# Three graph layers on one core: root products, late node blocks, lots and the last run are placed anew

## The chip, the cores and the metric

The kernel runs on one core of one Trainium2 chip. The metric is the device time of one execution in microseconds (us); the figure before is the median of three runs.

## The reference

A graph with 6250 nodes of 256 features and 100000 edges, sorted by destination. Destinations are crowded at low node numbers (`dst = 6250 * u**2`). Each edge has 32 attributes and one of three types. Three layers are computed, and a layer norm of the input plus the result stands at the end:

```python
ew = edge_attr @ edge_w + edge_b                      # 100000 x 256, the same for all layers
for l in range(3):
    msg = relu(x[src] * ew)
    out = 0
    for i in range(3):                                # mean over the edges of each type
        h = segment_sum(msg * (edge_type == i), dst) / max(count_i, 1)
        out = out + h @ weights[l, i]
    x = x + relu(out + x @ roots[l] + biases[l])
result = layernorm(x_in + x)
```

## The kernel before, in words

**Edges.** 256 edges make a pair (two tiles of 128), two pairs a quad; there are 391 pairs, numbered in the order of destinations. For each tile POOL issues one indirect gather, which fetches the 128 source rows into `xs` (L1378). A quad of rows has one of eight buffers (`ROWS = 8`). DVE multiplies a quad by the edge weights (`weigh`, L838), ACT applies relu (L839), DVE makes one-hot tiles of the destinations (`one_hot`, L852), and PE sums the rows into PSUM with them (`reduce`, L870 and L878). Consecutive pairs whose destinations fit into a window of 40 nodes form a run. A long run is first summed in the other orientation and turned (`take`, `turn`: the "turned" runs), and DVE adds each run to the accumulator `acc` (`add`, L918).

**Layer by layer.** Layer one also computes the edge weights on PE (`make_ew`, L815). It stores them for the later layers (`keep_ew`, L765 and L771), and it sorts the rows of the first 52 pairs by source block: each such tile is scattered by an indirect DMA from POOL to a table in memory (`scatter`, one after each later gather, L733). Layers two and three don't gather these 52 pairs. They read the table back in 39 "lots" (three types by 13 groups of four node blocks), whose source rows PE picks out of `x_all` in SBUF (`choose`, `expand`, L794, L801). A lot takes a quad's two steps and no gather.

**Nodes.** The nodes form 49 blocks of 128. When all of a block's edges are in `acc`, three products with the relation weights follow (`node_mul`, L947, in two parts), DVE scales and adds them (`node_end`, L978, L981) and SP writes the block to `x_mid` (L984). ACT clears its place in `acc`. The product with the root matrix comes earlier: `root_turn`, `root_turned`, `root_mul`, `root_keep` at steps s, s+2, s+3 and s+6 (L923, L927, L931, L934), into one of 22 slots (`ROOTS`). In the last layer a block is also normalised and stored (`deviate`, `norm`).

**Order.** `layer` is one loop over steps `it`. Each step emits work of many stages: the gather of pair `it + 9`, the product of pair `it + 3`, the reduction of pair `it`, and node work by table. Each engine executes its instructions in the order of emission and waits on semaphores, so POOL can run ahead of the other engines as far as buffers and scatters let it. `order_of` puts the pairs in order: 76 to 390 (with the sorted quads, or the lots, mixed in by `places_of`), then 75 down to 58, which belong to node block 1. `stages` says at which step each run is taken, turned and added; `schedule` gives `starts[c]`, the step in which block c's node products begin. Block 1 begins last, after the last run.

**Between layers.** The next layer gathers from `x_mid`. Its first six pairs (12 gathers, `gather_early`) are ordered so that they need all blocks but block 1, whose rows `complete` adds by a matmul. They are emitted after the last gather of a layer. From the seventh pair on, gathers read all of `x_mid`, block 1 included.

Of the kernel before, what the change touches and what calls it, by code (L numbers as in the profile page):

```python
# [442 lines left out]
def ordered_path(ctx, tc, x, attr_laid, A, weights, roots, biases, edge_w, edge_b, out, src, src_i, seg, place_i, consts, x_root,  # L443
# [8 lines left out]
    N, D = x.shape  # L452
    E = src.shape[0]
    L, R = weights.shape[:2]
# [230 lines left out]
    def layer(l, r_sb, b_sb, ats, early, pools):  # L685
# [5 lines left out]
        steps = len(order)  # L691
        soon = min(SOON, steps - max(starts[:1] + starts[2:]) - 5)
        taken, turns, added, banks = stages(N, E, share, l)
# [315 lines left out]

        node_at = {s: c for c, s in enumerate(starts)}  # L1010
        turns_of = [node_at[s] for s in sorted(node_at)]
        at_root = {c: (j + 2 * FIRST) % ROOTS for j, c in enumerate(turns_of)}
        root_at = {}

        for j, c in enumerate(turns_of):
            step = max(3 + int((steps - 110) * (1 - (1 - j / NT) ** 0.5)), max(root_at, default=-1) + 6)
            if j >= ROOTS:
                step = max(step, starts[turns_of[j - ROOTS]] + 5)
            assert step + 8 <= starts[c]
            root_at[step] = c  # L1020
# [6 lines left out]
        if l == L - 1:  # L1027
# [6 lines left out]
            for c in turns_of:  # L1034
                step = max(used[c], max(given_at, default=0) + 2)
                assert step <= starts[c] + 2, (c, step, starts[c])
                given_at[step] = c
        for it in range(-11, max(starts) + 8):
# [69 lines left out]
            if it - 2 == moved:  # L1108
                clear(P)
            if it - 2 in node_at:  # L1110
                node_end(node_at[it - 2], 0)
            if it - 4 in node_at:
                node_end(node_at[it - 4], 1)
                if node_at[it - 4] == 1:
                    node_end(1, 2)
                clear(slot_of(node_at[it - 4]))
            if it + 1 in node_at and slot_of(node_at[it + 1]) == 0:
                wrap()
            if it in node_at:
                node_mul(node_at[it], 0)  # L1120
            if it - 2 in node_at:
                node_mul(node_at[it - 2], 1)
                if node_at[it - 2] == 1:
                    node_mul(1, 2)
            if it - 5 in node_at and l == L - 1:
                deviate(node_at[it - 5])
            if it - 6 in node_at and l == L - 1:
                norm(node_at[it - 6])
            if pair(2) is not None and first_of(it + 2, 2) and pair(2) // 2 != order[-1] // 2:
# [44 lines left out]
LOT_AT = 6  # L1174
LOT_SPACE = 4.5
LOT_MORE = 0.04
LOT = 4
# [46 lines left out]
def places_of(N, E):  # L1224

    K = first_pairs(N, E)
    quads = [K + ZONE_AT + int(ZONE_SPACE * j) for j in range(zone_of(N, E) // 2)]
    lots = [K + LOT_AT + int(LOT_SPACE * j + LOT_MORE * j * j) for j in range(len(lots_of(N)))]
    return [w + w % 2 for w in quads], [w + w % 2 for w in lots], K + MIDDLE_AT


def spans_of(N, E):
# [6 lines left out]
    quads, lots, middle = places_of(N, E)  # L1239
    stops = {K, last, middle, *quads, *lots}  # L1240
    node = lambda e: N * min(1.0, e / E) ** 2
# [47 lines left out]
def stages(N, E, share, l):  # L1289
# [15 lines left out]
    for k, group in enumerate(groups):  # L1305
        done = closes[group[-1]]
        late = k + 2 < len(groups)
        some = any(turned(spans[n], last) for n in group)
        by = min(opens[groups[k + 2][0]] - 1, done + (4 if some else 3)) if late else 0
        by = max(by, done + 1 + some)  # L1310
        for j, n in enumerate(group):
# [6 lines left out]
            elif late and j < len(group) - 1:  # L1318
                added[s] = max(done + 1, by - 1)
    return taken, turns, added, banks  # L1320


def schedule(N, E, share, l):
# [23 lines left out]
    for c in range(2, NT):  # L1347
        if starts[0] is None and ready <= max(done[c] + 2, step + 4):
            step = starts[0] = max(ready, step + 4)
        step = starts[c] = max(done[c] + 2, step + 4)  # L1350
    if starts[0] is None:
# [214 lines left out]
```

## Time and profile before

| | us |
|---|---|
| median of three runs (2900.62 to 2906.98) | 2903.43 |
| profiled execution | 2903.96 |
| its span, first to last instruction | 2902.2 |
| gathers and scatters on POOL, number | 2242 |
| POOL busy | 2138.6 |
| PE busy | 2409.1 |
| DVE busy | 2207.5 |
| ACT busy | 1708.1 |
| mean granted TensorE clock | 0.948 of full speed |

In the rows that follow, a row of the timeline gives the start of an instruction in us from the start of the span, its duration, engine, line, operation, destination and source, and in brackets how long the engine had been idle before it and what released it. A row of the windows gives a stretch, its length, and for each engine the busy time with the number of instructions, then the granted clock. A row of the waits gives the total, the count and the longest.

### The profile page before, as it was taken

The page shows a single profiled execution, that of the slowest core. Times are in us where ns is not written, and L with a number is a line of the kernel's source. Part 1 is how long each engine was busy: PE and PEld are TensorE (multiplying, and loading weights), DVE is VectorE, ACT ScalarE, POOL GpSimd, SP SyncE. Part 2 cuts the span into 40 slices and gives each one's busy share as a digit, 9 for nine tenths or more (in the row PEclk, how much of TensorE's full clock was granted, in tenths as well). Part 3 has the DMA queues.
Part 4 walks back from the last instruction along what each step waited for, and adds up shares of the span by engine and source line. Part 5 has one row for each costly group of instructions (what it writes and reads, how often), then busy time and mean ns, then how long its engine had stood idle before and what let it go on. Part 6 is the DMA issues. An engine that isn't in the chain of part 4 may idle for free. (4 is left out here: it accounts for less than half of the span.)

```text
span 2902.2 us, 44132 instructions
## 1 busy us (share of the span) xinstructions
PE 2409.1 (83%) x13302; PEld 1880.6 (65%) x13302; DVE 2207.5 (76%) x5612; ACT 1708.1 (59%) x2220; POOL 2138.6 (74%) x2253
## 2 busy tenths in 40 slices
PE   5799988888988789788898888777888888878776
PEld 2466656555666566577777777665666767767665
DVE  7777766766656576677878888776788888888986
ACT  5677766666666667455655555444555555555654
POOL 7676777777777775777777777776777777767775
PEclk9899998999889999999999999898999999999998
DMA  7898665556555666887777777676777777777765
GB/s 237 280 328 272 207 198 190 189 185 196 185 192 187 196 211 202 267 262 240 256 242 243 246 237 257 215 223 195 269 255 262 255 256 240 244 227 233 249 227 156
DMA packets 285411, 668.25 MB, mean 230 GB/s; under 512 B 50555, under 2 KB 142509, under 8 KB 285165
## 3 DMA queue, kind: packets, MB, share of 16 engines
q1 hardware_dynamic: 170112, 362.98, 35.9%
q0 software_dynamic: 107616, 294.11, 33.9%
q10 hardware_dynamic: 7436, 8.24, 0.9%
q8 instruction: 110, 1.80, 0.3%
q14 instruction: 137, 1.11, 0.1%
HBM read 528.50 MB, written 136.63 MB: 229 GB/s over the span
## 5 line engine op out<-in xcount | busy, mean ns | idle before, releaser
L1378 POOL DMA_INDIRECT xs<-x_mid,src_r x1332 | 1265.3, 950 | 420.1 <-issue 343.1
L1378 POOL DMA_INDIRECT xs<-in_x_dram,src_io x770 | 734.9, 954 | 243.1 <-issue 211.8
L839 ACT ACTIVATE xs<-xs 128x1024 f32<-128x1024 f32 x533 | 559.5, 1050 | 582.8 <-DVE xs L838 561.0
L838 DVE TENSOR_TENSOR xs<-ew_p,xs 128x1024 f32<-128x1024 f32 x533 | 646.5, 1213 | 314.3 <-ACT keep L771 176.3
L878 PE MATMUL h_p<-oh,xs 128*128 128x120 f32 x4768 | 692.5, 293 | 202.7 <-DVE acc L918 105.4
L878 PEld LDWEIGHTS h_p<-oh,xs 128*128 128x128 f32 x4768 | 641.3, 203 | 304.9 <-DVE acc L918 112.4
L852 DVE TENSOR_SCALAR oh<-iota_w,seg_o 128x120 f32<-128x120 f32 x2138 | 568.2, 328 | 0.0
L870 PE MATMUL h_p<-xs,oh 128*120 128x256 f32 x1868 | 517.7, 405 | 41.5 <-issue 14.7
L947 PE MATMUL o_p<-w_sb,acc 128*128 128x256 f32 (+1 forms) x1752 | 456.1, 397 | 64.8 <-DVE x_root L978 56.6
L918 DVE TENSOR_TENSOR acc<-h_p,acc 128x240 f32 (+1 forms) x764 | 338.9, 445 | 113.5 <-PE o_p L947 45.7
L947 PEld LDWEIGHTS o_p<-w_sb,acc 128*128 128x128 f32 (+1 forms) x1752 | 323.6, 195 | 141.5 <-DVE x_root L978 73.9
L870 PEld LDWEIGHTS h_p<-xs,oh 128*120 128x120 f32 x1868 | 319.5, 189 | 146.6 <-issue 30.0
L786 ACT ACTIVATE ew_p<-ew_s 128x1024 f32<-128x1024 f32 (+1 forms) x340 | 343.3, 1010 | 12.7 <-DMA ew_s<-ew_all 12.7
L771 ACT ACTIVATE keep<-ew_p 128x1024 f32<-128x1024 f32 x170 | 173.2, 1019 | 226.1 <-issue 115.5
L978 DVE SCALAR_TENSOR_TENSOR x_root<-o_p,inv,x_root 128x256 f32<-128x256 f32 (+1 forms) x438 | 210.5, 480 | 43.0 <-PE o_p L947 36.1
L839 ACT ACTIVATE zone<-zone 128x1024 f32<-128x1024 f32 (+1 forms) x78 | 78.8, 1010 | 223.9 <-DVE zone L838 223.9
L815 PE MATMUL ew_p<-ew_sb,at 64*128 64x512 f32 x630 | 199.0, 710 | 11.8 <-ACT ew_p L789 11.7
L789 ACT ACTIVATE ew_p<-seed 128x1024 f32<-128x1024 f32 (+1 forms) x194 | 198.5, 1023 | 0.0
L931 PE MATMUL r_p<-r_sb,t_s 128*128 128x256 f32 x588 | 158.7, 392 | 21.7 <-ACT t_s L927 21.4
L838 DVE TENSOR_TENSOR zone<-ew_p,zone 128x1024 f32<-128x1024 f32 (+1 forms) x78 | 90.6, 1162 | 107.5 <-PE ew_p L801 107.3
L870 PE MATMUL h_p<-zone,oh 128*120 128x256 f32 x576 | 148.0, 387 | 11.6 <-DVE acc L918 7.0
L801 PE MATMUL ew_p<-x_all,hot 128*128 128x256 f32 x588 | 150.6, 401 | 7.6 <-DVE hot L794 7.4
(178 smaller groups left out, 2340.8 us busy)
## 6 DMA issues: line engine op xcount, KB each, us to landing
ew_s<-ew_all SPq DMA_DIRECT2D x338, 512.0 KB
ew_all<-keep SPq DMA_DIRECT2D x169, 512.0 KB
zone<-zone_table SPq DMA_DIRECT2D x72, 516.0 KB
xs<-x_mid,src_r POOLq DMA_INDIRECT x1332
zone_table<-blank SPq DMA_DIRECT2D x21, 677.2 KB
xs<-in_x_dram,src_io POOLq DMA_INDIRECT x770
x_mid<-x_all SPq DMA_DIRECT2D x96, 128.0 KB
at<-in_attr_laid_dram SPq DMA_DIRECT2D x40, 256.0 KB
```

Source lines behind the costliest of these rows:

```text
L786: nc.scalar.activation(ew_ps[q][:, :n], ew_ss[q][:, :n], AF.Copy)
L789: nc.scalar.activation(ew_ps[q][:, :n], seed[:, None, None, :].to_broadcast([P, n, 2, D]), AF.Copy)
L815: nc.tensor.matmul(ew_ps[q][:, k].rearrange("p i d -> p (i d)"), at[half, :], ew_sb[half].rearrange("p i d -> p (i d)"), start=False, stop ...
L838: nc.vector.tensor_mul(there, ew_ps[q][:, pairs.start:pairs.stop, :n], there)
L839: nc.scalar.activation(there, there, AF.Relu)
L852: nc.vector.tensor_scalar(ohs[q][:, i, :], iota_w[:, :, :WIN], at, None, op0=ALU.is_equal)
L870: nc.tensor.matmul(h_p[:WK, :D], ohs[u // 2][:, t, :], rows_of(u, i), start=(i == 0 and first), stop=(i == n - 1 and closes(u)), skip_grou ...
L878: nc.tensor.matmul(h_p[:, d * WK:(d + 1) * WK], rows_of(u, i)[:, d * P:(d + 1) * P] if d < DC else full_ones, (ohs if d < DC else oh_bs)[u ...
L918: nc.vector.tensor_tensor(there, h_ps[span][:, :CH * WK].rearrange("p (c r w) -> p c r w", c=CH, r=R), there, op=ALU.add)
L947: nc.tensor.matmul(o_p[:n, j, :], acc[:, d, r, slot:slot + n], w_sb[:, r * DC + d, :], start=(d == 0), stop=(d == DC - 1))
L978: nc.vector.scalar_tensor_tensor(root, o_p[:n, j, :], inv[:n, c, r:r + 1], root, op0=ALU.mult, op1=ALU.add)
L1378: nc.gpsimd.indirect_dma_start(out=xs[:, u % 2, i, :], out_offset=None, in_=x_rows[:, :], in_offset=bass.IndirectOffsetOnAxis(ap=src_i[:, ...
```

## The change

1. In layer one the root products are no longer placed at steps 5, 11, 17, ... 293 (every six), but at 20, 27, 34, ... 356 (every seven). The other two layers keep their rule.
2. The last five blocks (`QUICK = 5`, blocks 44 to 48) take one step instead of two between the parts of their node work (`paces`): part 0 at s, part 1 and the first end at s+1, the second end, the clearing and the write at s+2. Their starts may stand three steps apart instead of four (366, 369, 372, 375, 378 in layer one, where they stood at 366, 370, 374, 378, 382; 388, 392, 396, 399, 402 in the other two, before 388, 393, 397, 401, 405). Block 48 starts at step 378 instead of 382 in layer one and ends at 380 instead of 386; in layers two and three it starts at 402 instead of 405 and ends at 404 instead of 409.
3. The lots, up to the 26th at the same places within a few pairs, thin out after that: the last 13 stood at places 226 to 310 (226, 232, 240, 246, 254, 260, 266, 274, 282, 288, 296, 304, 310) and come to 230 to 342 (230, 238, 244, 252, 260, 270, 278, 288, 296, 306, 318, 330, 342). Block 0, which needs all lots, starts at step 352 instead of 319 in layers two and three.
4. The last run, 7 pairs (58 to 64), is cut into one of two pairs (58, 59) and one of six (60 to 65), which is turned. In layers two and three both are added at step 415 (before: 414), and block 1 starts at 416 instead of 415. The run of pair 390 is added as soon as it is complete.

```diff
@@ ordered_path, layer
-        soon = min(SOON, steps - max(starts[:1] + starts[2:]) - 5)
+        soon = min(SOON, steps - starts[0] - 5, *(steps - starts[c] - 2 * paces(c, NT) - 1 for c in range(2, NT)))
...
         node_at = {s: c for c, s in enumerate(starts)}
+        next_at = {s + paces(c, NT): c for s, c in node_at.items()}
+        over_at = {s + 2 * paces(c, NT): c for s, c in node_at.items()}
...
         for j, c in enumerate(turns_of):
-            step = max(3 + int((steps - 110) * (1 - (1 - j / NT) ** 0.5)), max(root_at, default=-1) + 6)
+            step = ROOT_AT + ROOT_EVERY * j if l == 0 else 3 + int((steps - 110) * (1 - (1 - j / NT) ** 0.5))
+            step = max(step, max(root_at, default=-1) + 6)
...
-            if it - 2 in node_at:
-                node_end(node_at[it - 2], 0)
-            if it - 4 in node_at:
-                node_end(node_at[it - 4], 1)
-                if node_at[it - 4] == 1:
+            if it in next_at:
+                node_end(next_at[it], 0)
+            if it in over_at:
+                node_end(over_at[it], 1)
+                if over_at[it] == 1:
                     node_end(1, 2)
-                clear(slot_of(node_at[it - 4]))
+                clear(slot_of(over_at[it]))
...
-            if it - 2 in node_at:
-                node_mul(node_at[it - 2], 1)
-                if node_at[it - 2] == 1:
+            if it in next_at:
+                node_mul(next_at[it], 1)
+                if next_at[it] == 1:
                     node_mul(1, 2)
-            if it - 5 in node_at and l == L - 1:
-                deviate(node_at[it - 5])
-            if it - 6 in node_at and l == L - 1:
-                norm(node_at[it - 6])
+            if it - 1 in over_at and l == L - 1:
+                deviate(over_at[it - 1])
+            if it - 2 in over_at and l == L - 1:
+                norm(over_at[it - 2])
...
-LOT_SPACE = 4.5
-LOT_MORE = 0.04
+LOT_RATE = 0.215
+LOT_SLOWER = 0.000264
+ROOT_AT = 20
+ROOT_EVERY = 7
+QUICK = 5
@@ places_of
-    lots = [K + LOT_AT + int(LOT_SPACE * j + LOT_MORE * j * j) for j in range(len(lots_of(N)))]
+    lots = [K + LOT_AT + int((LOT_RATE - (LOT_RATE ** 2 - 4 * LOT_SLOWER * j) ** 0.5) / (2 * LOT_SLOWER))
+            for j in range(len(lots_of(N)))]
@@ spans_of
-    stops = {K, last, middle, *quads, *lots}
+    stops = {K, last, last + 2, middle, *quads, *lots}
@@ stages
+        if spans[group[-1]][1] == -(-E // 256):
+            by = 0
         by = max(by, done + 1 + some)
+def paces(c, NT):
+
+    return 1 if c >= NT - QUICK else 2
@@ schedule
-        step = starts[c] = max(done[c] + 2, step + 4)
+        step = starts[c] = max(done[c] + paces(c, NT), step + 2 + paces(max(c - 1, 2), NT))
```

More of the change, by code (lines that the diff above doesn't have):

```diff
@@ L1035, in layer @@
                 step = max(used[c], max(given_at, default=0) + 2)
-                assert step <= starts[c] + 2, (c, step, starts[c])
+                assert step <= starts[c], (c, step, starts[c])
                 given_at[step] = c
```

## The prediction

> **What bounds the kernel now.** I read the page first, then POOL's waits, then its timeline where it stands still, and last the windows of the other engines there.
>
> ```profile
> span 2902.2 us, 44132 instructions
> POOL 7676777777777775777777777776777777767775
> L1378 POOL DMA_INDIRECT xs<-x_mid,src_r x1332 | 1265.3, 950 | 420.1 <-issue 343.1
> L1378 POOL DMA_INDIRECT xs<-in_x_dram,src_io x770 | 734.9, 954 | 243.1 <-issue 211.8
> ...
> 2880.84 0.95 POOL L1378 DMA_INDIRECT xs<-x_mid,src_r  x1 [0.30 <-issue]
> 2882.09 0.95 POOL L1378 DMA_INDIRECT xs<-x_mid,src_r  x1 [0.30 <-issue]
> ```
>
> PE has the most busy time, but POOL sets the pace: a gather lasts 0.95 us, the next follows 0.30 us later whatever the rest does, so one starts every 1.25 us, and a pair costs POOL 2.50 us. The sevens in POOL's slices are this pace (0.95/1.25 = 0.76). The 2242 gathers and scatters would fill 2242 x 1.25 = 2803 us. The first 4 us and the 20 us from the last gather's start (2882.09) to the end make 2827; the other 75 us of the span are gaps beyond 0.30 and a few longer gathers. The change removes no gather, so only the gaps and the end can give anything.
>
> ```profile
> 96.67 0.95 POOL L1378 DMA_INDIRECT xs<-in_x_dram,src_io  x1 [0.30 <-issue]
> 105.04 0.94 POOL L1378 DMA_INDIRECT xs<-in_x_dram,src_io  x1 [7.43 <-issue]
> ...
> 293.82 1.00 POOL L733 DMA_INDIRECT zone_table<-keep,slot_i  x1 [11.48 <-ACT keep L765]
> ...
> 1141.30 0.95 POOL L1378 DMA_INDIRECT xs<-in_x_dram,src_io  x1 [0.30 <-issue]
> 1159.06 0.94 POOL L1378 DMA_INDIRECT xs<-x_mid,src_e  x1 [16.81 <-DMA x_mid<-x_all]
> ...
> 1174.06 0.94 POOL L1378 DMA_INDIRECT xs<-x_mid,src_r  x1 [0.30 <-issue]
> ...
> 2007.43 0.95 POOL L1378 DMA_INDIRECT xs<-x_mid,src_r  x1 [0.30 <-issue]
> 2017.61 0.95 POOL L1378 DMA_INDIRECT xs<-x_mid,src_e  x1 [9.23 <-issue]
> ...
> 2032.60 0.95 POOL L1378 DMA_INDIRECT xs<-x_mid,src_r  x1 [0.30 <-ACT ew_p L786]
> ```
>
> Four gaps make 45 us: two in layer one's first tenth (a full set of row buffers, then the first scatter, which needs the edge weights of the first sorted quad) and one at each change of layer, where the early gathers wait for block 48 in memory. The rest, about 14 us, lies in layer three:
>
> ```profile
> 2300.00:2440.00 140.00, 119.62 (x667) 99.99 (x667) 118.18 (x299) 80.79 (x119) 105.87 (x113) 1.00 0.77 250
> 2440.00:2620.00 180.00, 145.37 (x923) 128.09 (x923) 156.16 (x403) 97.13 (x129) 125.56 (x133) 0.98 0.73 240
> ```
>
> 133 gathers in 180 us are 1.35 us each, against 140/113 = 1.24 just before: 180 - 133 x 1.25 = 14 us stood still.
>
> **Root products of layer one: 5 us.** The first scatter hangs on ACT's `keep_ew` for the quad at step 100, emitted at step 96. Up to there 16 root products were emitted (steps 5 to 95); now there are 11 (20 to 90). The stretch is close to PE's limit:
>
> ```profile
> 90.00:106.00 16.00, 5.48 (x17) 2.73 (x15) 8.07 (x30) 3.47 (x4) 6.73 (x8) 0.61 0.59 199
> 106.00:282.00 176.00, 161.78 (x845) 107.21 (x843) 137.77 (x365) 133.99 (x182) 132.30 (x140) 0.99 0.92 302
> ...
> L931 PE MATMUL r_p<-r_sb,t_s 128*128 128x256 f32 x588 | 158.7, 392 | 21.7 <-ACT t_s L927 21.4
> L923 PE MATMUL r_p<-ident_o,x_all x294: 270/273/475, 54.1 to 2676.9; 128*128 128x128 f32 x147
> ```
>
> A block takes 158.7/147 = 1.08 us of products and two overlapping transposes, at most 0.4 more by their 0.27 each. Five fewer save up to 5 x 1.4 = 7 us of PE before the scatter. PE is busy 162 of 176 us, and three of the five stand ahead of the stall at 90 to 106, so I take 5, with 0 and 7 as ends. The gap before the scatter shrinks from 11.5 to about 6 us. The nine products that now come at steps 300 to 356 (9 x 1.4 = 13 us of PE) lie beside scatters, where a pair costs POOL more; only the last two meet a full PE (below).
>
> **Late blocks and the first change of layer: 5 us, not 17.** What does the gap of 16.81 become?
>
> ```profile
> 1154.36 0.30 SPq L984 DMA_DIRECT2D x_mid<-x_all  x1
> 1164.58 0.34 SPq L984 DMA_DIRECT2D x_mid<-x_all  x1
> ...
> 1060.00:1100.00 40.00, 40.00 (x256) 29.84 (x256) 33.88 (x83) 31.73 (x37) 30.28 (x32) 1.00 0.73 236
> 1100.00:1155.00 55.00, 52.08 (x293) 36.01 (x290) 38.57 (x98) 42.22 (x52) 32.17 (x34) 1.00 0.67 216
> ```
>
> SP issues block 48's write at 1154.36, and 4.7 us later POOL starts (1159.06). Six steps earlier, at about 2.5 us a step, it would no longer hold POOL for 15 of the 16.8 us; PE's work for blocks 47 and 48 then comes first, so I expect the write some 9 to 12 us earlier. But the seventh pair needs block 1, whose write is issued at 1164.58 and lands, by the same 4.7, near 1169.3. Twelve early gathers last 15 us. Before, they ended at 1174.06, when block 1 had landed. Started earlier they end before it, and block 1 is late next: the gain is 1174.06 - 1169.3 = 4.8 us, if its write stays. PE was full from 1060 to 1155 (92 of 95 us), and moving work within a full stretch doesn't move its end; two late root products add up to 2.8 us there, and up to 2.9 us of idling may close. I take 5, with 1 and 9 as ends.
>
> What else moves with a block: SP's write goes ahead of the stores and loads of edge weights of some six steps, and waits there for DVE as it did before, no longer; the clearing on ACT comes earlier with it. The second part's products share one PSUM tile with the first's, so PE waits until DVE has scaled the first part:
>
> ```profile
> PE o_p L947 <- DVE x_root L978: 56.6, 53, 3.3
> ```
>
> That is 1.1 us a time. Scaling and second part are emitted in one step in both kernels, so I add nothing; if the first part's products are late for DVE at the closer pace, behind this wait stand PE's reductions, and for them DVE's additions: at most five more such waits a layer, 5 us, inside the ends above and below.
>
> **The second change of layer: 8 us.**
>
> ```profile
> 2012.66 0.25 SPq L984 DMA_DIRECT2D x_mid<-x_all  x1
> 2020.85 0.33 SPq L984 DMA_DIRECT2D x_mid<-x_all  x1
> ...
> 2009.00:2014.00 5.00, 5.00 (x40) 4.66 (x40) 3.77 (x11) 2.25 (x5) 0.00 (x0) 1.00 0.11 31
> ```
>
> Block 48 needed 2017.61 - 2012.66 = 4.95 us. Five steps earlier (12.5 us) it lands near 2005, before the last gather is issued (2008.7), so this gap can close. Block 1 lands near 2025.8; early gathers from 2008.7 end at 2023.7. With its write unmoved, 2032.6 - 2025.8 = 6.8 us are gained. Here PE was full only because block 48's chain (products, scaling, products) stood in it, and that leaves: I expect block 1 some 2 us earlier, less the price of the cut run, whose turning and second addition now stand between the last sum and block 1:
>
> ```profile
> L918 DVE TENSOR_TENSOR acc<-h_p,acc 128x240 f32 (+1 forms) x764 | 338.9, 445 | 113.5 <-PE o_p L947 45.7
> L890 PE MATMUL h_p<-ident_o,h_s 120*128 120x120 f32 x514 | 88.0, 275 | 1.4 <-ACT h_s L886 1.4
> ```
>
> An addition is 0.44 us, a turning two transposes of together 0.34 (88.0/257): 0.8. That makes 8; the ends are 5 and 8.9 (no gap).
>
> **Lots: 10 us in layer three.** How far the other engines lag behind POOL is the start of a quad's product minus that of its last gather. Pairs 238 and 294 (steps 224 and 296), then the end of the quad at 356 (step 361):
>
> ```profile
> 2443.58 0.94 POOL L1378 DMA_INDIRECT xs<-x_mid,src_r  x1 [0.30 <-issue]
> 2468.37 1.21 DVE L838 TENSOR_TENSOR xs<-ew_p,xs 128x1024 f32<-128x1024 f32 x1
> 2591.70 0.95 POOL L1378 DMA_INDIRECT xs<-x_mid,src_r  x1 [0.30 <-issue]
> 2621.94 1.22 DVE L838 TENSOR_TENSOR xs<-ew_p,xs 128x1024 f32<-128x1024 f32 x1
> 2640.77 1.22 DVE L838 TENSOR_TENSOR xs<-ew_p,xs 128x1024 f32<-128x1024 f32 x1
> 2754.03 0.94 POOL L1378 DMA_INDIRECT xs<-x_mid,src_r  x1 [0.30 <-issue]
> 2760.03 1.22 DVE L838 TENSOR_TENSOR xs<-ew_p,xs 128x1024 f32<-128x1024 f32 x1
> ```
>
> The lag is 24.8 us, then 30.2, and 6.0 once the lots are over. From step 305 (2640.77) to 361, 56 pairs without a lot take 119.3 us, 2.13 each, so 0.37 a pair is caught up. Between steps 224 and 296, 56 pairs and 8 lots take 153.6 us, so a lot costs (153.6 - 119.3)/8 = 4.3 us. POOL stood some 7 us in that time; without that the lag would be 37. The new places put 6 lots there: 37 - 8.6 = 28.6. POOL began to stand at about 25, so some 4 of the 14 us should remain: 10 gained. Ends: 4 (a lot at half its price) and 14. Three lots now follow, at 318 to 342, each beside 12 pairs that win back 4.4 us: the lag should stay near 25 and fall only after 342, where some 67 pairs are left, the last at a dense pace of blocks. I expect it nearly gone at the end of layer three and charge 2 us. Layer two has no standing in this part.
>
> **The end: 1 gained, 2 charged.**
>
> ```profile
> 2877.10 2.72 DMA xs<-x_mid,src_r
> ...
> 2886.65 0.75 DVE L844 TENSOR_TENSOR xs<-ew_p,xs 128x256 f32<-128x256 f32 x2
> ```
>
> A gather's rows were there 2.7 us after its start, so those of the last (2882.09) near 2884.8; the last product started at 2886.65, behind block 48's scaling on DVE. Up to 1.8 us go with block 48, less the 0.8 of the cut run. With the charge of 2 this part is -1, with ends of +2 and -5.
>
> **Sum.** 5 + 5 + 8 + 10 - 1 = 27 us of the profiled execution's 2903.96, so 2877; that execution lies 0.5 above the median of 2903.43, so 2876.4 for the median: 2876.
>
> **A rule against it.** The trace's clock falls where PE idles (0.61 at 90 to 106, PE busy 5.5 of 16 us), and stands at 1.00 at 2009 to 2014, with PE full. The steps after block 48 become emptier. If PE idles there, the strings between the last rows and block 1 (some 4 us of PE per layer) run at 0.61: 4 x (1/0.61 - 1) = 2.6 us, three times 8 us, so 2884. The Trainium skill, "TensorE: Matmul & The Clock Gate", Part 1, says that after an idle window of about 3.4 us the clock is halved. By that figure the loss would be an estimated 4 us per layer, 2888. The trace agrees that idling costs clock.
>
> **Rivals.**
> - *Block 1 comes much earlier* and both gaps close: 16.8 + 9.2 + 5 + 14 - 1 = 44 us, 2859. For it speaks that PE idled 2.9 us of 95, against it that PE has no more to give. 0.08.
> - *Clock*, as above: 2884. 0.07.
> - *The late lots keep the lag*: after place 342 nothing is caught up, because denser blocks eat the 0.37 a pair. Layer three ends with 22 us of lag where it now has 4.6 (last product 2886.65, last gather 2882.09): 17 lost, and 3 at the second change. 5 + 5 + 5 + 10 + 1 - 17 = 9, 2894. 0.12.
> - *The edits miss*: PE didn't set the scatter and block 1 holds both changes with its write late by 5: 0 + 0 + 3 + 4 - 1 = 6, 2897. 0.07.
> - *Slower*: after place 342 the blocks of three steps cost more than POOL's 2.50 a pair, and the lag grows to 30 us at the end of layers two and three. The second change then loses 16 (24 against the 8), the end 25: 5 + 5 - 16 + 10 - 25 = -21, 2924. It decides once a pair there costs over 2.50; the 2.13, with blocks every 4.7 steps, speaks against. 0.06.
>
> The forecast keeps 0.60.
>
> **Numbers.** The forecast's own range is 2868 to 2888. The range of 2862 to 2895 reaches to the lag's rival and leaves out most of the first, the miss and the slower one. About 0.2% (6 us) can be told from no change: faster 0.85 (forecast, first two rivals, most of the third), same 0.08, slower 0.07.
>
> **What would show it.** In the changed profile: the scatter's gap at 281 near 6 us; early gathers within 8 us of the last gather at the first change and at once at the second; a new gap behind the twelfth early gather, on block 1's write, of up to 7 us at the first change; POOL standing 4 us, not 14, in layer three; the last product within 7 us of the last gather. A last lag over 15 us, or new gaps at scatters between 900 and 1070, would make it wrong.

## The result: slower by 0.8%, and the profile after

The changed kernel takes 2927.39 us (median, 2921.9 to 2931.08), the kernel before on the same chip 2905.2 us (2900.62 to 2908.48): ratio 1.0076, 95% interval 1.0054 to 1.0098. I had forecast 2876 us, with 0.07 for slower. The profiled execution took 2921.9 us, 17.9 more than the profiled one before.

The page of the changed kernel (span, POOL's slices, the two groups of gathers):

```profile
span 2920.0 us, 44026 instructions
POOL 7676777777777776777777777777777776667774
L1392 POOL DMA_INDIRECT xs<-x_mid,src_r x1332 | 1268.9, 953 | 434.4 <-issue 357.3
L1392 POOL DMA_INDIRECT xs<-in_x_dram,src_io x770 | 737.4, 958 | 243.4 <-issue 210.6
```

The slice of the first change of layer (the sixteenth) reads 6 where it read 5, that of the second (the 28th) 7 where it read 6; late in layer three three slices in a row read 6 instead of one, and the last reads 4 instead of 5. POOL's timeline in the changed kernel, at the five places of which the prediction speaks:

```profile
281.78 0.95 POOL L1392 DMA_INDIRECT xs<-in_x_dram,src_io  x1 [0.30 <-DVE xs L838]
293.75 1.00 POOL L733 DMA_INDIRECT zone_table<-keep,slot_i  x1 [11.02 <-ACT keep L765]
...
1143.67 1.18 POOL L1392 DMA_INDIRECT xs<-in_x_dram,src_io  x1 [0.30 <-issue]
1157.34 0.95 POOL L1392 DMA_INDIRECT xs<-x_mid,src_e  x1 [12.49 <-ACT ew_p L789]
...
1171.13 0.95 POOL L1392 DMA_INDIRECT xs<-x_mid,src_e  x1 [0.30 <-issue]
1175.18 0.95 POOL L1392 DMA_INDIRECT xs<-x_mid,src_r  x1 [3.10 <-PE r_p L830]
...
2010.92 0.94 POOL L1392 DMA_INDIRECT xs<-x_mid,src_r  x1 [0.30 <-issue]
2012.17 0.95 POOL L1392 DMA_INDIRECT xs<-x_mid,src_e  x1 [0.30 <-issue]
...
2447.86 0.94 POOL L1392 DMA_INDIRECT xs<-x_mid,src_r  x1 [2.77 <-issue]
...
2462.06 0.95 POOL L1392 DMA_INDIRECT xs<-x_mid,src_r  x1 [4.47 <-ACT xs L839]
...
2889.38 0.95 POOL L1392 DMA_INDIRECT xs<-x_mid,src_r  x1 [0.30 <-issue]
```

The gap before the first scatter stayed (11.48 before, 11.02 now). At the first change the gap shrank from 16.81 to 12.49, and the new gap behind the twelfth early gather is there (3.10). The second change has no gap left. In layer three new gaps stand between 2440 and 2470. The last gather starts 30.6 us before the end of the span, where it was 20.1.

SP's queue in the changed kernel shows the writes of block 48 (1151.38) and block 1 (1172.66) at the first change, and both (the pair's first at 2004.82, the second ends at 2022.41) at the second:

```profile
1151.38 0.31 SPq L984 DMA_DIRECT2D x_mid<-x_all  x1
...
1172.66 0.32 SPq L984 DMA_DIRECT2D x_mid<-x_all  x1
...
2004.82 17.59 SPq L984 DMA_DIRECT2D x_mid<-x_all  x2
```

POOL issues its gathers and scatters in the same order in both kernels, so the starts of the n-th one (counted from 0) can be subtracted. The column "slower by" is the start in the changed kernel's trace less the start in that of before, "lost here" the growth since the row above, both taken before rounding:

| mark | before, us | after, us | slower by | lost here |
|---|---|---|---|---|
| first scatter (213) | 293.8 | 293.7 | -0.1 | -0.1 |
| last gather of layer one (885) | 1141.3 | 1143.7 | 2.4 | 2.4 |
| 14 gathers later (899) | 1175.3 | 1176.4 | 1.1 | -1.2 |
| last gather of layer two (1563) | 2007.4 | 2010.9 | 3.5 | 2.4 |
| first of layer three (1564) | 2017.6 | 2012.2 | -5.4 | -8.9 |
| 1900 | 2439.8 | 2435.4 | -4.5 | 1.0 |
| 2050 | 2642.7 | 2648.2 | 5.5 | 10.0 |
| last gather (2241) | 2882.1 | 2889.4 | 7.3 | 1.8 |
| end of the span | 2902.2 | 2920.0 | 17.9 | 10.6 |

Two places carry the loss: the stretch from the 1900th to the 2050th gather (the lots of layer three), and the end. The lag of the others behind POOL grew to 33.5 us at step 224, where it had been 24.8 (last gather of the quad, then its product):

```profile
2439.13 0.95 POOL L1392 DMA_INDIRECT xs<-x_mid,src_r  x1 [0.30 <-issue]
```
```profile
2472.66 1.22 DVE L838 TENSOR_TENSOR xs<-ew_p,xs 128x1024 f32<-128x1024 f32 x1
```

To see why, I took the stretch between the products of the quads at steps 184, 224 and 264, so that both kernels do the same 80 steps. The columns are as before: stretch, length, PE, PEld, DVE, ACT and POOL busy, granted clock, DMA share, GB/s. The kernel before:

```profile
2384.30:2468.40 84.10, 68.95 (x446) 60.39 (x445) 74.10 (x193) 45.36 (x60) 62.30 (x66) 1.00 0.76 250
2468.40:2549.10 80.70, 66.15 (x421) 58.67 (x422) 71.68 (x187) 44.83 (x60) 58.98 (x63) 0.98 0.75 244
```

The changed kernel:

```profile
2378.50:2472.70 94.20, 75.25 (x443) 66.70 (x441) 75.24 (x196) 46.09 (x61) 66.25 (x70) 0.91 0.69 225
2472.70:2558.80 86.10, 68.95 (x423) 61.60 (x424) 71.15 (x184) 44.50 (x58) 60.56 (x65) 0.94 0.73 239
```

866 matmuls instead of 867, and yet 180.3 us instead of 164.8. PE is busy 9.1 us longer and stands idle 6.4 us longer. The granted clock is either 1.0 or 0.5 in these traces, so by its column about 2 x (0.09 x 94.2 + 0.06 x 86.1) = 27 us of the changed kernel's stretch ran at half clock, against 2 x 0.02 x 80.7 = 3 us before. Half of the difference, 12 us, is the most that this can add to PE's busy time, so it is enough for the 9.1. (The mix of matmuls is not quite the same: the reductions of the edges, L878, are 504 instead of 488, the node products, L947, 119 instead of 110, the matmuls of the lots, L801 and L870, 129 instead of 149.)

### The profile page after: what moved, and what is told of

The parts are those of the page before. It is cut to its first block, busy times and chain, and to the rows that moved or that the text cites. A ratio compares the mean times of both kernels' runs of the same rounds, so it can differ in the third digit from the quotient of the medians.

```text
span 2920.0 us, 44026 instructions
## 1 busy us (share of the span) xinstructions
PE 2411.7 (83%) x13250; PEld 1887.9 (65%) x13250; DVE 2207.7 (76%) x5616; ACT 1710.4 (59%) x2223; POOL 2145.1 (73%) x2253
## 5 line engine op out<-in xcount | busy, mean ns | idle before, releaser
L878 PE MATMUL h_p<-oh,xs 128*128 128x120 f32 x4648 | 688.6, 296 | 217.4 <-DVE acc L918 106.8
L878 PEld LDWEIGHTS h_p<-oh,xs 128*128 128x128 f32 x4648 | 639.6, 205 | 310.3 <-issue 107.7
L870 PE MATMUL h_p<-xs,oh 128*120 128x256 f32 x1928 | 528.8, 403 | 60.2 <-issue 17.8
L947 PE MATMUL o_p<-w_sb,acc 128*128 128x256 f32 (+1 forms) x1752 | 458.6, 399 | 47.9 <-DVE x_root L978 42.8
L870 PEld LDWEIGHTS h_p<-xs,oh 128*120 128x120 f32 x1928 | 325.8, 187 | 177.7 <-issue 51.0
L947 PEld LDWEIGHTS o_p<-w_sb,acc 128*128 128x128 f32 (+1 forms) x1752 | 326.7, 197 | 124.1 <-DVE x_root L978 56.1
L786 ACT ACTIVATE ew_p<-ew_s 128x1024 f32<-128x1024 f32 (+1 forms) x340 | 343.4, 1010 | 11.5 <-DMA ew_s<-ew_all 11.4
L815 PE MATMUL ew_p<-ew_sb,at 64*128 64x512 f32 x630 | 199.1, 710 | 16.1 <-ACT ew_p L789 15.6
L870 PE MATMUL h_p<-zone,oh 128*120 128x256 f32 x576 | 150.3, 391 | 8.2 <-DVE acc L918 6.1
L801 PE MATMUL ew_p<-x_all,hot 128*128 128x256 f32 x588 | 151.1, 401 | 5.9 <-DVE hot L794 5.9
```

Of the source, the lines that this page charges most:

```text
L786: nc.scalar.activation(ew_ps[q][:, :n], ew_ss[q][:, :n], AF.Copy)
L815: nc.tensor.matmul(ew_ps[q][:, k].rearrange("p i d -> p (i d)"), at[half, :], ew_sb[half].rearrange("p i d -> p (i d)"), start=False, stop ...
L870: nc.tensor.matmul(h_p[:WK, :D], ohs[u // 2][:, t, :], rows_of(u, i), start=(i == 0 and first), stop=(i == n - 1 and closes(u)), skip_grou ...
L878: nc.tensor.matmul(h_p[:, d * WK:(d + 1) * WK], rows_of(u, i)[:, d * P:(d + 1) * P] if d < DC else full_ones, (ohs if d < DC else oh_bs)[u ...
L947: nc.tensor.matmul(o_p[:n, j, :], acc[:, d, r, slot:slot + n], w_sb[:, r * DC + d, :], start=(d == 0), stop=(d == DC - 1))
```

## The experiments

All runs but the last three fell on chips where the kernel before takes 3.91 to 3.97 ms; the last three fell on one where it takes 2905 us, as in the first comparison. On the slower chips DVE, ACT and POOL are busy for nearly the same time (DVE 2215.7 us against 2207.7 in the changed kernel's first trace), PE, at a mean granted clock of 0.834, for 2665.7 us against 2411.7, and all of them stand more. The changed kernel's page from such a chip:

```profile
span 3977.8 us, 44026 instructions
...
PE   4777665665565565866767767766667777677676
...
POOL 5555444445444445546555555566565555555663
```

In this trace PE, DVE and ACT stand still together for over 2 us at 94 places, 524 us in all; in the changed kernel's first trace it is 3 places and 12 us. The cause of that standing stays open. So I use these chips for ratios and for places, not for single microseconds.

**One part at a time.** The kernel before with the lots alone moved, three times; the other three parts alone:

```diff
# e1_lots, f_lots, h_lots: only
-    lots = [K + LOT_AT + int(LOT_SPACE * j + LOT_MORE * j * j) ...]
+    lots = [K + LOT_AT + int((LOT_RATE - (LOT_RATE ** 2 - 4 * LOT_SLOWER * j) ** 0.5) / (2 * LOT_SLOWER)) ...]
# e2_quick, h_quick: only QUICK = 5 (paces), e3_roots: only ROOT_AT, ROOT_EVERY, e4_cut: only
-    stops = {K, last, middle, *quads, *lots}
+    stops = {K, last, last + 2, middle, *quads, *lots}
...
+        if spans[group[-1]][1] == -(-E // 256):
+            by = 0
```

> Only the lots stand at their new places; root products, blocks and the last run are as before. Theory L (the lots moved late are what costs): POOL stands 22 to 28 us in layer three instead of 14, the last product comes over 10 us after the last gather instead of 4.6, and the time is 12 to 25 us above before. Rival (the lots help, as forecast, and the loss comes from the blocks or their mixture): POOL stands under 10 us in layer three and the time is 3 to 10 us below before.

> Only the last five blocks take one step between their parts. Theory Q (blocks in a full PE): at the end of layer one the lag of the products behind the gathers rises to about 20 us, block 1's write is 5 to 8 us later and the first change of layer gains nothing; the second change gains 6 to 9 us since PE has room there; layer three stays as before: 3 to 9 us below before. Rival (the dense blocks are what holds layer three's end): the end after the last gather grows from 20 to 26 us or more and the time is not below before.

> Only the root products of layer one stand at their new steps. Theory R0 (the front of layer one isn't bound by PE's root products): the first scatter starts at 293.8 us within 0.5 us, as before, and the late products cost 0 to 3 us at the end of layer one: 0 to 3 us above before. Rival (the forecast: PE sets the scatter): it starts 3 us or more earlier and the time is 2 to 6 us below before.

> Only the last run is cut in two and the run of pair 390 is added at once. Theory: within 2 us of before, up to 1 us more at each of the three ends for the turning and the second addition. Rival (the cut run holds up block 1 at the layer's end): block 1's write comes 4 us or more later at both changes and the time is 5 to 10 us above before.

Measured: lots 1.0033 [1.0006, 1.0061], blocks 0.9996 [0.9974, 1.0017], root products 0.9984 [0.9957, 1.001], cut 1.0 [0.9973, 1.0027]. Only the lots lie outside no change, on the slow side.

These traces tell which part moves block 1's write at the first change of layer. The last gather of layer one and block 1's write, with the three-step blocks alone (e2_quick), then with the late root products alone (e3_roots):

```profile
1682.58 0.95 POOL L1388 DMA_INDIRECT xs<-in_x_dram,src_io  x1 [0.31 <-issue]
...
1728.31 0.32 SPq L984 DMA_DIRECT2D x_mid<-x_all  x1
```
```profile
1681.01 0.95 POOL L1389 DMA_INDIRECT xs<-in_x_dram,src_io  x1 [0.30 <-issue]
...
1722.75 0.34 SPq L984 DMA_DIRECT2D x_mid<-x_all  x1
```

The write follows 45.7 us behind the gather with the blocks and 41.7 with the root products. In all traces of these chips it is 43.5 to 49.8 us in the nine with three-step blocks in layer one, and 40.5 to 42.1 in the six without them.

**With and without the lots; blocks in layer two alone; more room between root products.**

```diff
# f_nolots: the changed kernel with the old line for lots
# f_quick2: the kernel before with
+    return 1 if c >= NT - QUICK and l == 1 else 2
# f_space7: the changed kernel with
-            step = max(step, max(root_at, default=-1) + 6)
+            step = max(step, max(root_at, default=-1) + 7)
```

> The changed kernel with the lots of layers two and three back at their old places; the other three parts stay. Theory A, the new places of the lots cause the loss: the 13 us that POOL stood longer in layer three and the 10.6 us at the end go, the 8.9 us of the second change and the 1.3 us of the first stay, the slightly longer gathers of layers one and two (about 5 us) stay: 5 us under the kernel before, ratio 0.998, with POOL standing about 14 us in layer three. Theory B, the three-step blocks and the late root products cause it, and the lots are innocent: still 15 to 24 us over the kernel before, ratio 1.005 to 1.008.

> The kernel before with the lots alone moved to their new places. Theory A (the lots cause the loss): 13 us more standing in layer three and 10 us more at the end, 20 to 24 us over the kernel before, ratio 1.007 to 1.008. Theory B: no slower than before, ratio 0.997 to 1.001. My prediction's step said 10 us faster in layer three and 2 lost at the end, ratio 0.997.

> The kernel before with three-step blocks in layer two alone; root products, lots and the last run as before. If the 8.9 us of the second change belong to the blocks alone and nothing of it comes back later: 9 us under the kernel before, ratio 0.997, POOL's gap at the second change gone. Rival: the denser blocks leave the engines further behind POOL at the end of layer two, and layer three's standing takes the gain back: ratio 1.000.

> The changed kernel with at least seven steps instead of six between two root products in all layers, so that the product of one block is copied out before the turned block of the next wants its one PSUM buffer. Theory C, PE's short waits for that buffer pull the clock down and with it the lag up: the 81 us of weight-load waits at that buffer fall below 20, half-clock stretches between 2200 and 2550 us fall from ten to five or fewer, and the run is 5 to 15 us under the changed kernel, 2912 to 2922. Rival: the waits go elsewhere and the time stays within 4 us of the changed kernel's 2927, ratio 1.006 to 1.009 to the kernel before.

Measured: without the new lots 0.9954 [0.9928, 0.998], the lots alone 1.0041 [1.0016, 1.0066]. By their signs theory A holds and theory B (the blocks cost it) falls; both sizes were expected for a chip at 2.90 ms (0.998, and 1.007 to 1.008). Blocks in layer two alone 1.0009 [0.998, 1.0038], unclear, and the gap at the second change did not close on this chip (15.9 us). More room 0.9981 [0.9957, 1.0004].

**The changed kernel itself, the first scatter, and candidates.**

```diff
# g_noroots: the changed kernel, with root_turn, root_turned and root_mul left out
# in layer one for the products before step 104
# g_cand: f_nolots, with
+    return 1 if c >= NT - QUICK and l < 2 else 2
# g_cand7: g_cand with at least 7 steps between root products
```

> The changed kernel itself, beside the others of this call. If the loss belongs to the kernel and not to one chip, it is again slower than the kernel before, ratio 1.003 to 1.008. If it hangs on the clock that the first chip granted, the ratio lies within 1.000 to 1.002 on a chip that grants another clock.

> The changed kernel, which in layer one leaves out the turning, the copy and the products of the first 11 blocks' root products (those before step 104; the bias alone is kept, by one DVE copy each). My prediction's step, PE's root products hold up the first scatter: eight of them lie between POOL's stop for row buffers and the scatter's weights, 8 x 1.08 = 8.6 us or more, so POOL's gap before the first scatter (11.0 us in the changed kernel's first profile) falls to 3 us or less. Rival, something else sets the scatter (rows or stores in memory, or the ring of PE, ACT and DVE that one quad passes): the gap stays within 3 us of that of the changed kernel in this call.

> The changed kernel with the lots back at their old places and with three-step blocks in layers one and two alone, five-step ones in layer three. The second change's gain stays; the end should lose the lag that grew by 7 us over layer three's last 20 steps in the changed kernel, when the three-step blocks ran. If those blocks make that lag, the time from the last gather's start to the end is some 5 us shorter than with the changed kernel of this call and the ratio is 0.993 to 0.996. Rival, the lag at the end comes from the cut of the last run or from the clock: the end is as long as the changed kernel's.

> As g_cand, with at least seven steps between two root products in all layers. If PE's short waits for the one PSUM buffer of the root products cost time, 4 us or more under g_cand, ratio 0.992 or lower; if they only move elsewhere, within 0.1% of g_cand.

The changed kernel came to 1.0 [0.9974, 1.0025]: the loss of 0.8% is not seen on such a chip. There its gains and losses cancel, which f_nolots and the lots alone had pointed to. Without the 11 root products the gap before the first scatter is 14.07 us beside 15.58 in the changed kernel; the rival holds there. Nor do the even root products shorten it on these chips: it is 13.1 to 15.6 us in the seven other traces with them, and 12.7 to 15.6 in the seven with the old places. The candidate came to 0.9941 [0.9913, 0.9968], but its end was as long as the changed kernel's (41.5 and 40.8 us), so its own reason was not confirmed. With seven steps between root products it came to 0.9991 [0.996, 1.0021], worse, though the weight loads' waits for their buffer that end with DVE's copy (L934) had gone from 67.0 us to none in its list of waits. Theory C in that form is not borne out: the waits can be taken away, and the time does not follow.

**Again lots, candidate and blocks.**

> The kernel before with the lots alone moved. Theory A (the lots' new places cost the 24 us of the first comparison): on a chip where the kernel before takes 2.90 ms 13 us more standing in layer three and up to 10 us more at the end, ratio 1.007 to 1.008; on a chip where it takes 3.9 ms, as twice before, ratio 1.003 to 1.004, 13 to 16 us. Theory B (the blocks cost it): ratio 0.997 to 1.001.

> The same kernel as g_cand: old places of the lots, three-step blocks in layers one and two alone, even root products in layer one, the last run cut. On a chip where the kernel before takes 2.90 ms: the second change's 8.9 us and the first's 1.3 us stay, some 5 us go to longer gathers, and layer three and the end are as before: 5 us faster, ratio 0.998; if the lag at the end was the cut's, no faster, ratio 1.000 to 1.002. On a chip where it takes 3.9 ms: ratio 0.993 to 0.997 again.

> The kernel before with three-step blocks alone, in all layers. Where the kernel before takes 2.90 ms: if these blocks make the lag at the end of layer three, the end is 5 to 10 us longer while the second change gives 8.9 us, ratio 0.999 to 1.001; if they do not, ratio 0.997. The first change tells whether block 1's write comes 8 us later with the three-step blocks alone or only with the late root products beside them. Where it takes 3.9 ms: ratio 0.998 to 1.001 again.

Lots 1.0049 [1.0017, 1.008], candidate 0.9945 [0.9915, 0.9976], blocks 0.9984 [0.9958, 1.0009]. From the 1900th to the 2050th gather POOL took 243 to 253 us in the nine traces with old lots on these chips (mean 246.1), and 251 to 258 in the six with new ones (mean 255.9; 251 is the one with more room between root products). The 10 us of the first comparison stand in the same place.

**What of the lots costs.** Up to here it could be the thinning, the late lots, or only the steps at which lots meet other work. The last three runs, on a chip where the kernel before takes 2905.24 us:

```diff
# i_late: the changed kernel; lots 0 to 32 at the old places, the last six at the new ones
+    lots = [K + LOT_AT + int(4.5 * j + 0.04 * j * j) if j < 33 else K + LOT_AT + int((LOT_RATE - ...
# i_phase: f_nolots, all lots two steps later
-LOT_AT = 6
+LOT_AT = 8
# i_nocut: g_cand without the cut of the last run
-    stops = {K, last, last + 2, middle, *quads, *lots}
+    stops = {K, last, middle, *quads, *lots}
...
-        if spans[group[-1]][1] == -(-E // 256):
-            by = 0
```

> The changed kernel with the first 33 lots at their old places and only the last six at the new, late ones. In the profiles so far POOL needs 243 to 253 us from the 1900th to the 2050th gather in the nine kernels with old lots and 251 to 258 us in the six with new ones (203 and 213 on the first chip). Theory S, the shifted places from step 184 to 262 cost those 10 us, whose number is the same: that stretch takes 243 to 250 us, and the time is 8 to 12 us under the changed kernel, ratio 0.995 to 0.998. Theory T, the late lots cost it: stretch after it and the end longer, time as the changed kernel's, ratio 0.999 to 1.002.

> Root products, blocks and last run as in the changed kernel; the lots with the spacing of the kernel before, all two steps later. In steps 176 to 236 lots and blocks then stand within two steps of where the changed kernel has them, but nothing is thinned. Theory S in its narrow form (it is the meeting of lots, blocks and root products at these steps that costs, not how thin they are): the stretch from the 1900th to the 2050th gather takes 251 us or more, ratio 0.997 to 1.000. Rival, the thinning itself costs (blocks pulled forward by it, lots late): the stretch takes 243 to 248 us and the ratio is 0.994 to 0.997, as with old lots (0.9954 before).

> The kernel before with even root products in layer one and three-step blocks in layers one and two, the last run not cut. From the last gather's start to the end the four kernels with old blocks in layer three and no cut took 35 to 38 us, those with either 41 to 46. If the cut alone costs 5 us there and gives nothing else: 5 us under the same kernel with the cut, ratio 0.992 to 0.994. Rival, the cut gives at the changes of layer what it costs at the end: ratio 0.994 to 0.997.

Measured: i_late 2900.89 us, 0.9982 [0.997, 0.9993]; i_phase 2918.43 us, 1.0046 [1.0029, 1.0063]; i_nocut 2896.13 us, 0.997 [0.9959, 0.9982]. The last is the fastest of all: 9 us under the kernel before, where the changed one was 22 over it (in the first comparison; it was not run beside these three). The stretches and ratios in these expectations were taken from the slower chips, so here only their direction counts. The profiled execution of i_phase, 2908.09 us, is the fastest of its four and 10 us under their median.

The same 80 steps in i_late, then in i_phase:

```profile
2372.40:2456.70 84.30, 68.88 (x446) 60.36 (x444) 74.03 (x192) 45.20 (x60) 63.78 (x68) 1.00 0.76 251
2456.70:2537.30 80.60, 66.05 (x421) 58.56 (x422) 71.58 (x186) 44.75 (x60) 59.49 (x63) 0.98 0.73 241
```
```profile
2366.90:2461.20 94.30, 73.88 (x441) 65.12 (x440) 74.97 (x193) 45.76 (x61) 65.35 (x69) 0.93 0.68 223
2461.20:2547.30 86.10, 69.78 (x438) 61.80 (x438) 72.24 (x188) 43.97 (x58) 57.89 (x61) 0.96 0.72 236
```

164.9 us where the old places are kept, 180.4 where all lots stand two steps later and nothing is thinned. i_phase has 12 matmuls more than the kernel before in them (879 against 867, 2 us at 143.66/879 = 0.16 us each), the changed kernel one fewer. So such a loss needs neither more work nor thinning; it goes with the steps at which lots and other work meet: i_phase has lots at 176, 184, 194, 202, 210, 218 and blocks at 180, 187, 196, 206, 215, 225, the changed kernel lots at 176, 184, 194, 202, 212, 222 and blocks at 180, 187, 196, 206, 214, 223. Which meeting it is I did not isolate. One more thing moves with the lots: their places are among the `stops` at which a run must end, in every layer, so other runs are cut too (in layer three 9 of 286 in the changed kernel, 26 of 285 in i_phase and 4 of 286 in i_late are not runs of the kernel before). No run here keeps the old runs and moves the lots.

POOL's way through layer three, from differences of gathers' starts as above:

| us | before | after | i_late | i_phase | i_nocut |
|---|---|---|---|---|---|
| 1900 to 2050 | 202.8 | 212.8 | 194.3 | 217.2 | 200.8 |
| 2050 to the last | 239.4 | 241.2 | 243.9 | 239.6 | 239.8 |
| last gather to the end | 20.1 | 30.6 | 29.2 | 26.1 | 21.3 |

i_late shows what the late places of the last six lots do: 8.5 us won in the stretch and 4.5 lost behind it, where i_phase loses 0.2. At its end it loses 9.1, 3.2 more than i_phase, which has the same blocks and cut run. The last gather and the last product of i_late, and the last product of the changed kernel:

```profile
2867.92 0.95 POOL L1392 DMA_INDIRECT xs<-x_mid,src_r  x1 [0.30 <-issue]
```
```profile
2879.39 0.75 DVE L844 TENSOR_TENSOR xs<-ew_p,xs 128x256 f32<-128x256 f32 x2
```
```profile
2901.79 0.74 DVE L844 TENSOR_TENSOR xs<-ew_p,xs 128x256 f32<-128x256 f32 x2
```

The lag at the last gather is 11.5 us in i_late, 12.4 in the changed kernel (2901.79 - 2889.38); in i_phase, with the same blocks and cut but no late lots, it is 8.0, in i_nocut 5.9, before 4.6. So of the 7.9 us of lag more in the changed kernel, about 4 come with the late lots and about 3 with the three-step blocks and the cut run. On the slower chips the lag at the last gather is 20.0 to 21.2 us with the lots alone, against 19.9 and 21.4 where lots, blocks of layer three and last run are all old; it is 25.3 and 25.2 with the blocks alone and 24.9 with the cut alone. So the blocks and the cut each make lag at the end, and the share of the lots rests on the traces above. From the last product to the end it is 18.2 us in the changed kernel, 17.8 and 18.0 in i_late and i_phase, 15.4 in i_nocut and 15.5 before: the cut and the three-step blocks of layer three, which these runs don't part, cost 2.2 to 2.9.

The first scatter's gap in these three runs:

```profile
289.12 1.00 POOL L733 DMA_INDIRECT zone_table<-keep,slot_i  x1 [6.92 <-ACT keep L765]
```
```profile
286.72 0.99 POOL L733 DMA_INDIRECT zone_table<-keep,slot_i  x1 [3.88 <-ACT keep L765]
```
```profile
287.12 1.00 POOL L733 DMA_INDIRECT zone_table<-keep,slot_i  x1 [8.07 <-ACT keep L765]
```

All three have the root products of the changed kernel, whose gap was 11.02, but not its front: since the lots' places also end runs, 5 of the 42 runs added before step 108 end elsewhere in the changed kernel than before, and 22 of 41 in i_phase. i_late and i_nocut have the runs of the kernel before and, up to the first scatter, the same order of instructions on PE, DVE and ACT as each other; their gaps differ by 1.2 us. Beside the kernel before, from which only the places of the root products part them up to there, the gap is 4.6 and 3.4 us shorter.

## Why the prediction was wrong

*Second change of layer: 8 forecast, 8.9 measured, right.* Block 48's write is issued at 2004.82, where it was at 2012.66, and the early gathers follow the last gather at once. i_late and i_phase gain 8.9 as well, i_nocut, without the cut, 6.5. On the slower chips the gap stays (15.9 to 19.9 us in the ten traces with three-step blocks in layer two, 19.2 to 22.9 in the five without).

*First change: 5 forecast, 1.2 measured, within its ends of 1 and 9.* The step that failed is "if its write stays". Block 1's write is issued 29.0 us after layer one's last gather starts (1172.66 - 1143.67), where it was 23.3 (1164.58 - 1141.30); block 48's, for which I expected 9 to 12 us, came 5.4 earlier against that gather (7.7 us behind it, 13.1 before). In the three last runs it is 28.5 to 30.8, and their gain from layer one's last gather to 14 gathers later is -0.6 to +0.6 us. The end of the full stretch did move, by some 6 us, and took back what block 48 gave. On the slower chips it is the three-step blocks that do it, and not the late root products beside them (45.7 us with the blocks alone, 41.7 with the root products alone): pulling blocks forward in a full stretch put off block 1.

*Root products: 5 forecast, 0.1 measured, not settled.* i_late and i_nocut, with the new places and the old runs of layer one, have gaps 4.6 and 3.4 us shorter than the one profile before, near the forecast; in the changed kernel, where the new lots also end 5 of the first runs elsewhere, that gain is missing. On the slower chips the gap hangs neither on the places of the products nor much on 11 of them being there. One profile of each kernel was too little for a term of 5 us here, and I had not seen that the lots reach into layer one.

*Lots: 10 to be gained in layer three, 11.8 lost (10.0 and 1.8).* This is the term that turned the sum. I gave each lot a price of 4.3 us and took the price to be the same wherever the lot stands. That is the step that failed. i_late, where the first 33 lots keep their steps, still gains: 8.5 us in the stretch less 4.5 behind it, 4 of the 10. But the new places also moved the lots of those 80 steps by two to ten steps and the blocks by up to four, and i_phase shows that a move of two steps, with what it does to runs and blocks, costs 15 us over 80 steps with next to the same work. The price itself had a wrong reading under it: the steps from 305 to 361 don't hold 56 pairs and no lot, but 54 pairs and two lots of one node block each (at 307 and 314); if these two cost nothing, a pair takes 2.21 us and a lot 3.7. The three lots that I put at 318 to 342 are of that small kind too. This would have changed the term by about 1 us, not its sign. I had looked at how many lots a stretch holds, not at what each one meets. None of my rivals had this.

*The end: -1 forecast, -10.6 measured.* Its ends of +2 and -5 didn't hold it. My rival "the late lots keep the lag" is seen in small part: in i_late the lag of 28.2 us at step 336 is caught up to 8.7 at step 391, where i_phase, without late lots, has 3.0. So the charge of 2 us was too small, but most of the lag went as forecast. My slower rival, blocks of three steps that cost more than POOL's 2.50 a pair, is seen in part: in the changed kernel the lag falls to 7.4 us at step 391 and then rises to 14.6 at step 408, in i_phase from 3.0 to 10.3. The last gather of the quad and its product in the changed kernel, first at step 391, then at 408:

```profile
2836.57 0.95 POOL L1392 DMA_INDIRECT xs<-x_mid,src_r  x1 [0.30 <-issue]
...
2843.98 1.22 DVE L838 TENSOR_TENSOR xs<-ew_p,xs 128x1024 f32<-128x1024 f32 x1
```
```profile
2879.36 0.95 POOL L1392 DMA_INDIRECT xs<-x_mid,src_r  x1 [0.30 <-issue]
...
2894.01 1.21 DVE L838 TENSOR_TENSOR xs<-ew_p,xs 128x1024 f32<-128x1024 f32 x1
```

This rival named the right sign and, by chance, nearly the right time (2924); its loss of 16 us at the second change did not come. From the last product to the end 2.2 to 2.9 us more go with the cut and the three-step blocks, where I had charged 0.8 for the cut.

*Left out of the sum:* POOL lost 2.4 us each in the long even parts of layers one and two; its mean gather is 958 ns instead of 954 in layer one and 953 instead of 950 in the other two. The three last runs lose 0.5 to 2.2 and up to 1.7 there.

*Clock.* I had it as a rival at 2884, at the ends of layers. It came in the middle of layer three instead (0.91 and 0.94 over the 80 steps, against 1.00 and 0.98 before).

## What to carry to other kernels

In this kernel several in-order engines share a hand-written order and PE is busy for 83% of the span, and there a mean price per lot did not hold once the lots changed their steps. So move such items in an order that is otherwise unchanged, and price the shift by itself first (here two steps cost 14 us between the 1900th and the 2050th gather). Look also at what else is derived from their places, as the ends of runs are here. Test parts of a change alone before joining them; here blocks in layers one and two with even root products give 9 us, and the rest of the change takes back 31. And when work is put off, look at what is left at the end to catch up in, and at what that end costs itself.

## What the runs showed of the hardware

In these traces the clock falls without a long idle time. PE in the changed kernel, then the windows of the same stretch, cut where the granted clock changes:

```profile
2429.67 0.44 PE L923 MATMUL r_p<-ident_o,x_all 128*128 128x128 f32 x2 [2.66 <-DVE x_root L934]
...
2431.88 1.92 PE L878 MATMUL h_p<-oh,xs 128*128 128x120 f32 x8
...
2437.15 1.05 PE L878 MATMUL h_p<-oh,xs 128*128 128x120 f32 x8
```
```profile
2427.40:2430.80 3.40, 1.03 (x7) 0.82 (x8) 3.40 (x10) 1.99 (x4) 2.48 (x4) 1.00 0.66 193
2430.80:2434.20 3.40, 3.06 (x16) 2.81 (x15) 2.12 (x6) 1.21 (x2) 2.48 (x4) 0.50 0.99 375
2434.20:2437.60 3.40, 3.40 (x25) 3.19 (x26) 1.06 (x5) 0.88 (x2) 2.76 (x3) 0.99 0.90 320
...
2451.30:2454.70 3.40, 0.99 (x5) 0.89 (x6) 2.74 (x8) 1.42 (x3) 2.49 (x4) 1.00 0.74 250
2454.70:2458.10 3.40, 3.40 (x13) 2.73 (x11) 3.37 (x12) 2.30 (x4) 2.27 (x3) 0.50 0.56 161
```

A wait of 2.66 us leaves PE busy for 1.03 of 3.4 us; the next 3.4 us run at half the clock, and eight matmuls take 1.92 us where they take 1.05 at full clock. The half-clock stretches lie on a grid of 3.413 us in all traces. I sorted the windows of this grid in the five traces of the chips at 2.9 ms that ran at full clock by how long PE was busy in them. Of 302 with PE busy under 0.45 of the window, 257 are followed by a window at half clock; of 168 between 0.45 and 0.55, 52; of 3347 above 0.55, none. The Trainium skill, "TensorE: Matmul & The Clock Gate", Part 1, says that the clock falls after an idle window of about 3.4 us; the grid agrees, but here half an idle window is enough. So in these traces short waits that fall into one window cost the next one half its speed, and this goes with the lots' new places: between 2200 and 2620 us 11 such stretches begin in the changed kernel and 8 in i_phase, against 4 before, 3 in i_late and 5 in i_nocut. That the fall makes up the loss, and doesn't only go with it, is argued from the 9.1 us of longer matmuls; no run took it away by itself.
